# A gated cross-attention layer with routed experts: constants, buffers, a scaling step and PSUM banks moved

## Chip, core and metric

The kernel runs on one core of a Trainium2 chip. The metric is the device time of one execution in microseconds (us); lower is better. A core has TensorE for matmuls (PE in the profile, with its weight loads as PEld), VectorE (DVE), ScalarE (ACT), GpSimd (POOL) and SyncE (SP), which here only issues DMAs. Each engine works through its own queue in order; semaphores hold an instruction until what it needs is there. SBUF is the memory on the core; PSUM takes the results of matmuls, in eight banks of 512 fp32 values a partition.

## What is computed

For 8 batches of 512 tokens of width 256, one layer in fp32: attention of the normalized tokens `x` over a context of 512 keys with 16 heads of 16, masked, then a mixture of 8 experts of which each token takes 2. Both parts are added to `x` through a gate.

```python
x = x + tanh(g_xattn[0]) * attn(layernorm(x), ctx_1024, ctx_1024, mask, wq, bq, wk, bk, wv, bv, wo, bo)
x = x + tanh(g_ffn[0]) * ffn(layernorm(x), router_w, router_b, expert_up, expert_down)

# attn
scores = einsum("bhqd,bhkd->bhqk", q, k) / sqrt(16)
scores = where(mask == 0, -1e9, scores)
out = einsum("bhqk,bhkd->bhqd", softmax(scores), v) @ wo.T + bo
# ffn
probs = softmax(x_flat @ router_w + router_b)
top_w, top_idx = top_k(probs, 2)
output = sum over e of comb[:, e] * (gelu(x_flat @ expert_up[e].T) @ expert_down[e].T)
```

The drawn mask keeps the same keys, fewer than 128 in a row, for every query; the kernel finds this out on the chip and then attends only to a window of 128 keys.

## The kernel before

**The mask stage** (lines 95 to 585) loads the mask (`mask_i`, L98) and the first batch's tokens, makes constants on VectorE and POOL, and counts the dropped keys: `dropped` (L434, VectorE), its sum over rows `n_ps` (L446, TensorE), `act` (L447). From `act` and the constants `ahead` (L397, L398, made of `keys`) it reduces the first key `first` (L452) and the place of the window, `window_i` (L459), which SP reads into a register for the DMA of the keys' window (`load_window`, L467). `here`, `kept`, `diag`, `row_ps`, `drop` and `pick` (L490 to L503) describe which keys of the window count. `near_i` (L523) says whether the window covers all kept keys. Meanwhile `norms_0` measures the first batch's tokens: `look` (bn_stats, L209) and `settle` (L214 to L230, twelve small operations in a chain that ends in `rstd_end` and `shift`). Batch 0's projections end the stage: `kv_ps` (L537), `xnT_ps` (L259), `k_ps` (L549), `q_ps` (L568). The temporaries of this stage (`mask_i`, `dropped`, `xnT_0` and others) lie in the pool `mk`, which is given back at its end. A pool that is allocated over such memory makes its first users wait until the last reader of the old tiles is done.

A branch on `near_i` (L1349) then chooses `attend_near`, which is all that runs here; the other side, `attend_anywhere`, doesn't run.

**Pools of `attend_near`** (L806 to L823), in order of allocation in SBUF: `p2` (tokens `x`, windows `win`, `xnT`, weights' transposes `pT` and others), `small`, an empty pool `hold`, and then those that `experts` makes (`plan`, `weights`, `gather`, `hT`). In PSUM: `ps_s` with 4 banks (scores `t_ps` and `w_ps`, and the experts' `h_ps`), `ps_g` with 2 (everything else: `kv_ps`, `xnT_ps`, `q_ps`, `top_ps`, `proj_ps`, `bias_ps`, `o_ps`), `ps_o` with 2 (head outputs `n_av`, and `x_ps`, the transposed rows of an expert group).

**Rounds.** A loop over b from -1 to 7 (L1036) runs four groups g in each round, each for a half c of the heads and one parity i. In a group: `weights_T` (L891, four matmuls `w_ps` into four banks, each read by ScalarE's Exp, L903), `weigh` of the group before (L908: `n_av`, then VectorE's transpose `raw`, L922, and a division), `find_tops` of the next batch (L859: eight matmuls `t_ps` into four banks, each read by VectorE's max `tops`, L873), and `lower_tops` (L880: `top_ps`, then `ql`, L887). Between them stand the steps that `between` (L952) hands out by group and place `(g, n)`: projections of batch b+2, statistics and settle of b+3, output projection (`project_out`, L933) and routing (`route`, L304) of b-1. `scale_out` (L836) multiplies the output weights `woT` and bias `bo` by the gate: two matmuls into `bias_ps` (L844) with `bv_rows` (L843) as weights, and VectorE's L845, L847 and L846. `add_bias` (L849) adds `bo` to a batch's `x` on POOL (L850). Both run first at the end of round -1.

```python
if new == 1:
    put(3, 2, scale_out, lambda: add_bias(0))
put(*((3, 2) if new == 1 else (2, 0)), bias)
```

`new` is the batch that is being prepared, b+2 in round b; it is 1 in round -1.

**Experts.** Routed tokens are sorted into groups of 256 rows of one expert. Each group gathers its rows from DRAM (`xg`, L706), turns them (`x_ps`, L722, copied to `xT` by VectorE, L724), goes up (`h_ps`, L734, Gelu on ScalarE, L738) and down (`o_ps`, L752), is added to gathered rows of the output (`y`, L755) and scattered (L758). `plan` (L600) makes tables of which group is whose; its first instruction on VectorE is a memset of `groups` (L627). Some groups run within rounds 4 to 7 (`amid`, L1012), the rest in a loop after them.

**Order.** The program is written in order, and the scheduler of the tile framework may move an instruction on its engine where data allow it; `keep_in_program_order` pins one. SP's DMAs keep their order: mask, weights, first window, small constants, then window and tokens of batches 1 and 2, a clear of the routing table, and further tokens and windows.

Of the kernel before, what the change touches and what calls it, by code (L numbers as in the profile page):

```python
# [10 lines left out]
F32 = mybir.dt.float32  # L11
# [4 lines left out]
ALU = mybir.AluOpType  # L16
AX = mybir.AxisListType
PSUM = bass.MemoryType.PSUM

P = 128  # L20
B, S, D = 8, 512, 256
H, DH = 16, 16
# [4 lines left out]
EPS = 1e-5  # L27
# [36 lines left out]
def flamingo_layer(ctx: ExitStack, tc: tile.TileContext, a: dict, out: bass.AP):  # L64
    nc = tc.nc
# [5 lines left out]
    def fixed(shape, name, dtype=F32):  # L71
        return const.tile(shape, dtype, tag=name, name=name)
# [102 lines left out]
    ones_b = mk.tile([P, P], BF16, tag="ones_b", name="ones_b")  # L175
    nc.vector.memset(ones_b, 1.0)

    filled = keep.tile([P, E], F32, tag="filled", name="filled")
    nc.vector.tensor_scalar(filled, iota, float(TOKENS), None, ALU.mult)

# [13 lines left out]
    def measure(small, jobs, pin=False):  # L194


        nm = "_".join(f"{which}{b}" for b, which in jobs)
        n = len(jobs) * QT
        said = {}

        def column(name, i=0):
            return small.tile([P, 2 * QT], F32, tag=name, name=f"{name}_{nm}_{i}", bufs=3)[:, :n]

        def look(k):
            if "mv" not in said:
                said["mv"] = small.tile([P, 2 * QT, 2], F32, tag="mv", name=f"mv_{nm}", bufs=2)
            for t in range(QT):
                st = small.tile([P, 6], F32, tag="st", name=f"st_{nm}_{k}_{t}", bufs=4)
                ins = nc.vector.bn_stats(st, xs[jobs[k][0]][:, t, :])  # L209
                if t == 0 and pin:  # L210
                    tc.keep_in_program_order(ins)
                nc.vector.bn_aggr(said["mv"][:, k * QT + t, :], st)

        def settle():  # L214
            mv = said["mv"]
            v = column("var")
            nc.vector.tensor_scalar(v, mv[:, :n, 1], EPS, None, ALU.add)
            y = column("rstd")
            nc.vector.tensor_scalar(y.bitcast(I32), v.bitcast(I32), -0.5, RSQRT_MAGIC, ALU.mult, ALU.add)
            for i in range(3):  # L220
                yy = column("yy", i)
                nc.vector.tensor_tensor(yy, y, y, ALU.mult)
                hv = column("hv", i)
                nc.vector.scalar_tensor_tensor(hv, yy, -0.5, v, ALU.mult, ALU.mult)
                y2 = column("rstd", i + 1) if i < 2 else column("rstd_end")
                nc.vector.scalar_tensor_tensor(y2, hv, 1.5, y, ALU.add, ALU.mult)
                y = y2
            shift = column("shift")
            nc.vector.scalar_tensor_tensor(shift, mv[:, :n, 0], -1.0, y, ALU.mult, ALU.mult)
            said["rstd"], said["shift"] = y, shift  # L230

        return said, [lambda k=k: look(k) for k in range(len(jobs))], settle
# [178 lines left out]
    qs = [fixed([P, DC, S], f"q{i}") for i in range(2)]  # L411
    ks, kms = ([fixed([P, DC, 2, WINDOW], f"{n}{i}") for i in range(2)] for n in ("k", "km"))

    vals = [fixed([P, H, 2 * DH], f"nv{i}") for i in range(3)]
    for t in vals:
        nc.vector.memset(t[:, :, DH:], 1.0)

    act = mk.tile([P, S], F32, tag="act", name="act")
    first = fixed([P, 1], "first")
    window = fixed([P, 1], "window")  # L420
# [2 lines left out]
    with early, tc.tile_pool(name="ps_mask", bufs=1, space=PSUM) as ps_mask:  # L423
# [13 lines left out]
        norms_0 = measure(const, [(0, "a")], True)  # L437
# [35 lines left out]
        for dst, src in (  # L473
# [6 lines left out]
            (bv, a["bv"].partition_broadcast(P)),  # L480
        ):
            tc.keep_in_program_order(nc.sync.dma_start(out=dst, in_=src))
        norms_0[2]()

# [19 lines left out]
        for i in range(2):  # L506
            ins = nc.vector.tensor_scalar(bks[:, i, :], bk, half[:, 1 - i : 2 - i], None, ALU.mult)
# [298 lines left out]
    def attend_near(att):  # L806

        pool = lambda name, bufs, **kw: att.enter_context(tc.tile_pool(name=name, bufs=bufs, **kw))
        p2 = pool("near2", 2)
        small = pool("near_small", 4)  # L810
        hold = pool("near_hold", 1)
        ps_s = pool("near_ps_s", 4, space=PSUM)
        ps_g = pool("near_ps_g", 2, space=PSUM)
        ps_o = pool("near_ps_o", 2, space=PSUM)

        def bank(name):
            return ps_g.tile([P, 512], F32, tag="g", name=name)

        layernorms, finish = shared(p2, small, bank)
        plans, list_rows, fetch, load, turn_rows, ups, fetch_y, downs, compute, compute_extra = experts(  # L820
            pool, [b * S for b in PARTS], lambda name: ps_s.tile([P, 512], F32, tag="s", name=name), bank,
            lambda name: ps_o.tile([P, 512], F32, tag="av", name=name),
        )  # L823

        def held(shape, name, dtype=F32):
            return hold.tile(shape, dtype, tag=name, name=name)

        wins = {}

# [19 lines left out]
        def add_bias(b):  # L849
            nc.gpsimd.tensor_tensor(xs[b], xs[b], bo.unsqueeze(1).to_broadcast([P, QT, D]), ALU.add)  # L850
# [101 lines left out]
        def between(old, new, next_):  # L952

            plan = {(g, n): [] for g in range(4) for n in range(3)}

            def put(g, n, *steps):
                plan[g, n] += steps

            jobs = []
            if old is not None:
                x2T, keep_x, keep_rows, logits, route, place = finish(old)
                jobs.append((old, "f", x2T))
            if next_ is not None:
                xnT[next_] = None
                jobs.append((next_, "a", lambda: xnT[next_]))
            if jobs:
                looks, settle = normalize(*jobs)
            if new is not None:  # L970
                keys_values, keys_T, keys_less, bias, queries = prepare(new)
                _, scales, turns = normal[new, "a"]
                put(0, 2 if new == 1 else 0, keys_values)
                put(0, 1, *scales)
                put(1, 1, *turns, keys_T)
                put(3, 0, keys_less)
                put(2, 0, queries[0])
                put(2, 1, queries[1])
                if new == 1:
                    put(3, 2, scale_out, lambda: add_bias(0))  # L980
                put(*((3, 2) if new == 1 else (2, 0)), bias)
            if next_ is not None:
                put(0, 2, looks[-1])
            if old is not None:
                rows_f, scales, turns = normal[old, "f"]
                put(0, 1, lambda: project_out(old, (0, 1)))
                put(1, 0, lambda: project_out(old, (2, 3)), keep_x)
                put(1, 1, looks[0])
            if jobs:
                put(1, 2, settle)  # L990
            if old is not None:
                put(2, 0, *scales)
                put(2, 2, lambda: keep_rows(rows_f()))
                put(3, 0, *turns)
                put(3, 1, logits)
                put(3, 2, route)
                place, *enter = place
                counts = [count for count, end in zip(plans, PARTS) if old + 1 == end]
                later.append((place, enter, counts))
            return plan  # L1000
# [31 lines left out]
        looks, settle = normalize((1, "a", lambda: xnT[1]))  # L1032
# [3 lines left out]
        for b in range(-1, B):  # L1036
# [8 lines left out]
            if b == 0:  # L1045
                looks, settle = normalize((2, "a", lambda: xnT[2]))
# [11 lines left out]
            for g in range(4):  # L1058
                c, i = g // 2, g % 2
# [289 lines left out]
    with tc.If(is_near == 1) as which, ExitStack() as att:  # L1349
        attend_near(att)  # L1350
# [66 lines left out]
```

## Time and profile before

| | |
|---|---|
| device time, median of 3 runs | 852.25 us (850.71 to 857.43) |
| the profiled execution's own time | 827.52 us |
| its span, first to last instruction | 825.8 us |
| mean granted clock of TensorE | 0.974 |
| busy: PE, PEld | 763.0 us (92%), 571.9 us (69%) |
| busy: DVE, ACT, POOL | 317.8 us (38%), 252.6 us (31%), 313.6 us (38%) |
| TensorE, `h_ps` and `o_ps` together | 245.2 + 243.7 us |
| HBM | 147 GB/s over the span |

How to read it: the page's slices show each engine's busy share in tenths, over 40 equal parts of the span. The windows sum busy time in a stretch, with the number of instructions (x) and the granted clock (1.00 is full). A timeline line has start, length, engine (SPq is SP's queue), line of the kernel, operation, written and read tile, shape, count, and in brackets the idle time of the engine before it with what ended it. A matmul counts as busy while it waits in TensorE's pipeline, so a group of matmuls that takes longer than its like has waited.

### The profile page before, as it was taken

How to read it: one execution, taken by the hardware profiler on the slowest of the kernel's cores; microseconds unless marked ns; L12 is line 12 of the kernel's file. 1: busy time of each engine (PE TensorE's matmuls, PEld its weight loads, DVE VectorE, ACT ScalarE, POOL GpSimd, SP SyncE). 2: the span in 40 equal slices, each digit the busy share in tenths (PEclk: the TensorE clock that was granted, in tenths of full speed). 3: DMA queues.
4: the chain of work that ended last, by engine and by line, in shares of the span. 5: the costliest groups of instructions: out<-in, count | busy, mean ns of one | idle time of the engine just before them, and what ended most of it. 6: DMA issues, size and time to landing. Idle time of an engine off the chain costs nothing. (4 is left out here: it accounts for less than half of the span.)

```text
span 825.8 us, 11292 instructions
## 1 busy us (share of the span) xinstructions
PE 763.0 (92%) x4090; PEld 571.9 (69%) x4090; DVE 317.8 (38%) x958; ACT 252.6 (31%) x485; POOL 313.6 (38%) x422
## 2 busy tenths in 40 slices
PE   2788999998999899999996999999999999999992
PEld 1344545454465666768785888888898988989881
DVE  7468789888873565633320011111111101101100
ACT  1435475563644244442321121111211121111210
POOL 2021106244453251645464443443353433443331
PEclk9887999999999999999998999999999999999997
DMA  4610011120663214154548565665666775756511
GB/s 141 230 50 1 23 37 36 52 81 19 217 216 104 66 62 121 57 176 144 167 144 305 163 219 199 201 227 170 231 198 212 233 239 185 259 179 238 204 46 37
DMA packets 87909, 121.58 MB, mean 147 GB/s; under 512 B 16797, under 2 KB 71712, under 8 KB 87840
## 3 DMA queue, kind: packets, MB, share of 16 engines
q1 hardware_dynamic: 75184, 93.44, 33.8%
q0 software_dynamic: 11840, 26.76, 10.5%
q8 instruction: 36, 0.59, 0.3%
q10 hardware_dynamic: 816, 0.53, 0.2%
q14 instruction: 33, 0.27, 0.1%
HBM read 101.05 MB, written 20.17 MB: 147 GB/s over the span
## 5 line engine op out<-in xcount | busy, mean ns | idle before, releaser
L734 PE MATMUL h_ps<-xT,up 128*128 128x256 f32 (+1 forms) x1152 | 245.2, 370 | 5.9 <-DVE tops L873 4.3
L752 PE MATMUL o_ps<-down,hT 128*128 128x256 f32 x1088 | 243.7, 382 | 5.9 <-DVE y L755 5.5
L734 PEld LDWEIGHTS h_ps<-xT,up 128*128 128x128 f32 x1152 | 209.7, 191 | 35.7 <-DVE tops L873 5.1
L752 PEld LDWEIGHTS o_ps<-down,hT 128*128 128x128 f32 x1088 | 205.4, 192 | 37.1 <-DVE y L755 5.7
L738 ACT ACTIVATE hT<-h_ps 128x512 f32<-128x512 f32 (+1 forms) x144 | 82.2, 573 | 362.4 <-PE h_ps L734 362.3
L755 DVE SCALAR_TENSOR_TENSOR y<-o_ps,listed,y 128x256 f32<-128x256 f32 x68 | 32.7, 483 | 271.6 <-DMA y<-out,listed 133.3
L706 POOL DMA_INDIRECT y<-out,listed x68 | 66.1, 972 | 162.4 <-DMA out<-y,listed 130.6
L758 POOL DMA_INDIRECT out<-y,listed x68 | 68.8, 1012 | 95.6 <-DVE y L755 62.1
L873 DVE TENSOR_REDUCE tops<-t_ps 128x4 f32<-128x512 f32 x128 | 79.4, 680 | 18.2 <-PE t_ps L868 18.2
L903 ACT ACTIVATE n_pT<-w_ps 128x512 f32<-128x512 f32 x128 | 67.4, 598 | 44.4 <-PE w_ps L898 44.2
L706 POOL DMA_INDIRECT xg<-rows,listed x68 | 65.2, 958 | 40.4 <-issue 17.2
L372 POOL DMA_INDIRECT table<-entries,place_i x64 | 62.7, 979 | 25.9 <-issue 16.4
L898 PE MATMUL w_ps<-ql,km 32*128 32x512 f32 x256 | 62.8, 655 | 3.9 <-DVE tops L873 3.9
L724 DVE COPY xT<-x_ps 128x512 f32<-128x512 f32 (+1 forms) x36 | 23.6, 657 | 105.3 <-PE x_ps L722 105.3
L868 PE MATMUL t_ps<-k,q 32*128 32x256 f32 x512 | 43.9, 416 | 3.0 <-DVE tops L873 2.2
L868 PEld LDWEIGHTS t_ps<-k,q 32*128 32x128 f32 x512 | 27.1, 191 | 25.3 <-issue 15.0
L850 POOL TENSOR_TENSOR x<-x,bo 128x1024 f32<-128x1024 f32 x8 | 18.7, 2348 | 65.7 <-ACT xn_a L249 36.8
L898 PEld LDWEIGHTS w_ps<-ql,km 32*128 32x128 f32 x256 | 24.8, 187 | 19.7 <-DVE tops L873 15.0
L922 DVE STREAM_TRANSPOSE raw<-n_av 128x512 f32<-128x512 f32 x32 | 22.8, 712 | 34.3 <-PE n_av L916 34.3
L916 PE MATMUL n_av<-n_pT,nv 128*32 128x512 f32 x256 | 35.0, 619 | 0.0
L937 PE MATMUL proj_ps<-woT,oT 128*128 128x256 f32 x128 | 32.9, 392 | 1.6 <-DVE oT L930 1.5
L568 PE MATMUL q_ps<-n_xnT,wqT 128*128 128x512 f32 x64 | 32.9, 641 | 0.0
(187 smaller groups left out, 542.0 us busy)
## 6 DMA issues: line engine op xcount, KB each, us to landing
up<-in_upT SPq DMA_DIRECT2D x36, 1024.0 KB, 7.7
down<-in_downT SPq DMA_DIRECT2D x36, 1024.0 KB, 6.3
out<-x SPq DMA_DIRECT2D x8, 512.0 KB, 3.1
rows<-xn_f SPq DMA_DIRECT2D x8, 512.0 KB, 3.8
x<-in_x SPq DMA_DIRECT2D x7, 512.0 KB, 5.3
table<-none SPq DMA_DIRECT2D x1, 2288.0 KB, 11.0
xg<-rows,listed POOLq DMA_INDIRECT x68, 4.3
y<-out,listed POOLq DMA_INDIRECT x68, 2.8
```

The lines of the kernel that those rows point to most:

```text
L372: nc.gpsimd.indirect_dma_start(out=table_parts[2 * t + i][:, :], out_offset=bass.IndirectOffsetOnAxis(ap=place_i[:, t, i : i + 1], axis=0) ...
L568: nc.tensor.matmul(ps, lhsT=w["wqT"][:, dc, c * P : (c + 1) * P], rhs=xnT[:, dc, :], start=(dc == 0), stop=(dc == DC - 1),)
L706: nc.gpsimd.indirect_dma_start(out=dst, out_offset=None, in_=src[: seen[JOBS[s][0]], :], in_offset=bass.IndirectOffsetOnAxis(ap=listed[:, ...
L734: nc.tensor.matmul(ps[:, i, :n], lhsT=up[:, dc, (f + i) * P : (f + i + 1) * P], rhs=xT[:, dc, :n], start=(dc == 0), stop=(dc == DC - 1),)
L738: nc.scalar.activation(made[s][:, f : f + 2, :n], ps[:, :, :n], AF.Gelu)
L752: nc.tensor.matmul(ps, lhsT=hT[:, f, h * P : (h + 1) * P], rhs=down[:, f, :], start=(f == 0), stop=(f == FC - 1))
L758: nc.gpsimd.indirect_dma_start(out=out_parts[h][:, :], out_offset=bass.IndirectOffsetOnAxis(ap=listed[:, n, h, 0:1], axis=0), in_=y[:, h, ...
L868: ins = nc.tensor.matmul(ps[j][:, u], lhsT=q[rows_j, c, t * P : (t + 1) * P], rhs=k[rows_j, c], start=True, stop=True)
L873: nc.vector.tensor_reduce(top[:, 2 * tp : 2 * tp + 2, :].rearrange("p t (i x) -> p t i x", i=2)[:, :, :, 32 * j], ps[j], AX.X, ALU.max,)
L898: ins = nc.tensor.matmul(ps[j], lhsT=km[rows_j, c, i, :], rhs=lowered[b, c][rows_j, i, :], start=True, stop=True)
L903: nc.scalar.activation(pT[:, j, :], ps[j], AF.Exp)
L916: ins = nc.tensor.matmul(av[32 * j : 32 * j + 32, :], lhsT=made_of(b)[3][:, 8 * c + 2 * j + r, :], rhs=pT[:, j, :], start=True, stop=True,)
```

## The change

Three things move, and two pool sizes change:

1. The buffers `vals` and their memsets are made beside the early constants, and the settle of the first batch's statistics is pinned to program order. In the changed program's order on VectorE, the constants (`iota_e`, `filled`, `half`, `own`, `keys`, `ahead`, `less`) stand ahead of the first `dropped`, `first` and `window_i` follow `act` directly, and all twelve operations of settle come after `window_i`. On TensorE the first half of `kv_ps` stands ahead of `row_ps`.
2. In `attend_near` the experts' pools are allocated first, then `p2` and `small`; the empty `hold` goes. The experts' buffers now lie over the mask stage's temporaries.
3. `scale_out` moves from the end of round -1 to `(0, 2)` of round 0, with `add_bias` of batches 0 and 1 at `(1, 0)` and `(1, 2)`; batch 2's stays at `(2, 0)` of that round. In TensorE's order, `bias_ps` stands ahead of the second group's `w_ps`, with two of the third batch's transposes between its two halves.
4. `ps_s` has 5 banks, `ps_o` has 1.

SP's and POOL's queues keep their order of instructions.

```diff
@@ mask stage
+    vals = [fixed([P, H, 2 * DH], f"nv{i}") for i in range(3)]
+    for t in vals:
+        nc.vector.memset(t[:, :, DH:], 1.0)
+
     filled = keep.tile([P, E], F32, tag="filled", name="filled")
...
-        def settle():
+        def settle(pin=False):
             mv = said["mv"]
             v = column("var")
-            nc.vector.tensor_scalar(v, mv[:, :n, 1], EPS, None, ALU.add)
+            ins = nc.vector.tensor_scalar(v, mv[:, :n, 1], EPS, None, ALU.add)
+            if pin:
+                tc.keep_in_program_order(ins)
...
-    vals = [fixed([P, H, 2 * DH], f"nv{i}") for i in range(3)]
-    for t in vals:
-        nc.vector.memset(t[:, :, DH:], 1.0)
-
...
-        norms_0[2]()
+        norms_0[2](True)
@@ attend_near
-        p2 = pool("near2", 2)
-        small = pool("near_small", 4)
-        hold = pool("near_hold", 1)
-        ps_s = pool("near_ps_s", 4, space=PSUM)
+        ps_o = pool("near_ps_o", 1, space=PSUM)
         ps_g = pool("near_ps_g", 2, space=PSUM)
-        ps_o = pool("near_ps_o", 2, space=PSUM)
+        ps_s = pool("near_ps_s", 5, space=PSUM)
...
-        layernorms, finish = shared(p2, small, bank)
         plans, list_rows, fetch, load, turn_rows, ups, fetch_y, downs, compute, compute_extra = experts(
...
-        def held(shape, name, dtype=F32):
-            return hold.tile(shape, dtype, tag=name, name=name)
+
+        p2 = pool("near2", 2)
+        small = pool("near_small", 4)
+        layernorms, finish = shared(p2, small, bank)
@@ between
-                if new == 1:
-                    put(3, 2, scale_out, lambda: add_bias(0))
-                put(*((3, 2) if new == 1 else (2, 0)), bias)
+                if new == 2:
+                    put(0, 2, scale_out)
+                    put(1, 0, lambda: add_bias(0))
+                    put(1, 2, lambda: add_bias(1))
+                if new > 1:
+                    put(2, 0, bias)
```

## Prediction

> **What bounds the kernel now.** I read the slices of the page first: they tell where a change can pay.
>
> ```profile
> span 825.8 us, 11292 instructions
> ...
> PE   2788999998999899999996999999999999999992
> PEld 1344545454465666768785888888898988989881
> DVE  7468789888873565633320011111111101101100
> ```
>
> A slice is 20.6 us. From slice 20 on (about 400 us) TensorE is full and VectorE nearly idle: there only matmuls count, and the change removes none. In the first 350 us VectorE has 6 to 9 tenths and TensorE's nines are busy with waiting too. All three edits work there. Next the windows, for that first part:
>
> ```profile
> 20.00:30.00 10.00, 8.19 (x39) 4.59 (x38) 1.40 (x7) 5.58 (x13) 0.85 (x5) 1.00 0.22 65
> 30.00:40.00 10.00, 6.68 (x26) 3.09 (x24) 8.03 (x28) 2.76 (x6) 0.00 (x0) 0.80 1.05 368
> 40.00:50.00 10.00, 9.54 (x46) 4.90 (x48) 2.75 (x5) 4.22 (x10) 0.00 (x0) 0.69 0.44 136
> 60.00:70.00 10.00, 6.42 (x23) 2.71 (x25) 8.97 (x32) 4.46 (x8) 3.55 (x2) 0.67 0.00 0
> 100.00:150.00 50.00, 48.20 (x320) 24.65 (x323) 42.61 (x126) 31.55 (x68) 13.57 (x24) 1.00 0.18 57
> ```
>
> After the stretch come busy times of PE, PEld, DVE, ACT, POOL, then the granted clock. VectorE is idle 8.6 of 10 us at 20 to 30, and the clock falls twice. Then the timeline at those places:
>
> ```profile
> 26.82 0.39 SPq L467 DMA_DIRECT2D win<-in_ctxT  x1
> 26.92 0.42 DVE L843 TENSOR_SCALAR bv_rows<-ones,bvT 128x128 f32<-128x128 f32 x1 [5.87 <-PE q_ps L568]
> 27.33 0.95 SPq L86 DMA_DIRECT2D x<-in_x  x2
> 31.44 0.75 DVE L209 BATCH_NORM_STATS2 st_a<-x 128x6 f32<-128x256 f32 x2 [4.10 <-DMA x<-in_x]
> ...
> 56.56 4.65 POOL L850 TENSOR_TENSOR x<-x,bo 128x1024 f32<-128x1024 f32 x2 [28.89 <-DVE bo L846]
> 58.17 0.76 DVE L217 TENSOR_SCALAR var_a<-mv_a 128x4 f32<-128x4 f32 x1
> 58.96 2.27 DVE L219 TENSOR_SCALAR rstd_a<-var_a 128x4 int32<-128x4 int32 x1
> 63.85 3.01 PE L898 MATMUL w_ps<-ql,km 32*128 32x512 f32 x6 [3.58 <-DVE tops L873]
> ...
> 110.93 2.45 DVE L873 TENSOR_REDUCE tops<-t_ps 128x4 f32<-128x512 f32 x4
> 111.78 2.77 PE L898 MATMUL w_ps<-ql,km 32*128 32x512 f32 x8
> 115.61 0.72 DVE L922 STREAM_TRANSPOSE raw<-n_av 128x512 f32<-128x512 f32 x1 [1.59 <-PE n_av L916]
> ```
>
> First, `x1` is issued at 27.33, when the first batch's `q_ps` are done (26.62), although the branch's flag `near_i` was made at 20.52: its buffer lies over the mask stage's. Second, `rstd_a` takes 2.27 us where it takes 0.17 elsewhere, beside POOL's adds. Third, eight matmul records that take 1.14 us elsewhere take 2.77: each `w_ps` takes the bank of a `t_ps` whose `tops` is being read, one per 0.60 us.
>
> **What the Trainium skill says.** "SBUF — State Buffer", section "Who interferes with whom": a VectorE instruction that can take two ports (tensor_scalar, copy, cast), or that has two SBUF inputs while GpSimd reads SBUF, blocks against a GpSimd instruction for its whole length. The trace agrees: `rstd_a` ends with POOL's add (61.23 against 61.20), and `n_o`, two SBUF inputs, takes 1.74 us at 235.87 beside such an add against 0.42. "TensorE: Matmul & The Clock Gate", section "What's actually happening": an idle window of about 3.4 us halves the clock. The trace has half clock from 36.0 to 46.2 and 63.3 to 73.6, the second just after TensorE's 3.6 us wait; the threshold itself no run here shows. "PSUM — Partial Sum Buffer", section "Specifications (TRN2)": 8 banks of 512 fp32 a partition. So 5 + 2 + 1 uses all, and the fifth bank is taken from `ps_o`; the trace shows no bank count.
>
> **The change part by part.**
> *Constants ahead of the mask.* By start-to-start spacing, the eleven constants between 11.28 and 13.82 take 1.7 us of VectorE. They now stand ahead of the first `dropped` (3.83), from 2.3 on, where VectorE is idle 1.5 us before it and 1.5 us after. POOL works there without a pause; port waits bound the delay between 0 and 1.2 us (two memsets of `tops` at 1.05 each, part hidden). I take 0.4. Then `first` follows `act` (10.31) at once: `window_i` is ready at 11.9 instead of 14.41 and the window's load goes 2.4 us earlier. But now the first half of `kv_ps` (1.9 us of 3.75) stands ahead of `row_ps` on TensorE, and `drop`, `pick`, `kept`'s users and `near_i` wait behind it: `row_ps` ends at 15.1 + 1.9 + 0.8 = 17.8, not 17.04, so `near_i` comes 0.8 later, at 21.3. TensorE's chain to `q_ps` ends 1.7 us earlier, at 24.9. The pinned settle is the same twelve operations, and `here` keeps its 14.3.
>
> *Groups' buffers over first temporaries.* `p2` no longer lies over the mask pool, so SP's loads lose that wait. SP came through the branch in 0.6 us (20.55 to 21.11), so `x1` issues at 21.3 + 0.6 + 0.5 = 22.4 instead of 27.33 and, at the 4.1 us of before, lands at 26.5 instead of 31.4. The wait for `q_ps` isn't gone: the memset of `groups` now carries it, ahead of the statistics on VectorE, but ends by 25.0. So `x1`'s load stays last, and statistics start 4.9 us earlier. From there to `t_ps` at 45.83 one chain runs (statistics, `xn_a`, transposes, `q_ps`), so this carries. I count **4.7**, bounds 3.7 and 5.2. The table's clear (2,288 KB, issued at 29.02) and the later loads go earlier with it, on the same queue in the same order.
>
> *Output weights in round 0.* `scale_out` leaves the end of round -1: between `ql`'s end (53.74) and the next statistics (56.38) 2.6 us go, and `var_a`/`rstd_a` lose 0.6 + 2.1 = 2.7 us of port waits. VectorE's chain to `tops` at 63.11 gains about 5.1. In round 0 it all comes back: `bv_rows` 0.3, a wait for `bias_ps` of about 0.7 (0.60 for the matmul), `bo`, `woT`, `bo` 1.1. And now POOL has three adds ready at once, since the third batch's `xn_a` is done by then: 3 x 2.34 = 7.0 us without a pause. Settle of the next `x` stands in it: statistics fit under the first add, `var` waits for the first to end, `rstd` for the second, `yy` (two SBUF inputs) for the third. That is about 4.9 us lost; 2.1 + 4.9 = 7.0. Net on VectorE a loss of 1.9, of which some is slack (VectorE sat idle 0.9 and 1.35 before `ql` and `raw` at 75 to 77). I take a loss of **1.5**, bounds a loss of 4 and a gain of 1.6 (no third collision). Late next is `tops` for `w_ps` of group (1,0).
>
> *Five banks, one.* With five, `w_ps` number j waits for the reduce of `t_ps` j-1: 0.60 us less per group whose four start staggered. In the timeline 14 of 32 groups do. It pays where VectorE then idles for `n_av` (five groups: the one above, its like in rounds 2 to 4, the first of round 1) or TensorE is the bound (four, at 269 to 316): 9 x 0.60 = 5.4. In the other five, routing work covers it. In the main loop TensorE has no gap to fill. One bank for `n_av` and `x_ps` costs where they overlapped: `n_av` at 342.49 must wait for `xT` to end (344.17), but `h_ps` waits for that `xT` too, so 1.0; at 364.66 for 365.11, 0.5. Net a gain of **3.9**, bounds -1.5 and 7.
>
> *The sum.* 4.7 - 1.5 + 3.9 = 7.1 us, off the profiled execution's 827.52 (span 825.8 and 1.7 around it): 820.4. The runs' median, 852.25, lies 24.7 us above that; the profile doesn't show why, so I carry the saving over as it is: **845.1**.
>
> **The rivals.**
> *All of it at once, faster by over 1%.* `x1` comes early enough that TensorE has no idle window before 36 us, so the half clock there goes (`q_ps` 3.62 against 1.98, transposes 2.16 against 1.09, `k_ps` 1.22 against 0.71: 3.2 us), and every staggered group pays (14 x 0.6 - 1.5 = 6.9) while the scaling costs nothing: 4.7 + 3.2 + 6.9 = 14.8, 837.5. For: TensorE waits 2.2 us for `tops` at 33.7 and 1.15 for `xn_a` just before the fall. Against: the row-tiled matmuls there fill little of the array whenever they come.
> *The single output bank makes it slower.* `x_ps` holds its bank until VectorE copies `xT`, and VectorE's queue stands up to 19.5 us (133.3 in all) in `y` updates that wait for gathered rows. Three holds in rounds 4 to 7 are 5.1, 9.7 and 3.3 us; if `n_av` comes at the start of each, TensorE loses 18.1, net +11: 863. It decides once such waits pass 15.6 us (8.5 and the 7.1 gained). For: the bound stage hides nothing. Against: in before only 0.9, 1.7 and 0.5 us of these holds overlapped, and the order puts `x_ps` no earlier.
> *It doesn't do what it says.* The memset of `groups` is held by something later than `q_ps`, VectorE starts where it did, and 3.9 - 1.5 is left, less the 0.4 and 0.8 by which the flag is late: 851.
>
> **How the numbers follow.** About 1%, 8.5 us, is what a measurement here can tell from no change. The forecast has 0.44, the full gain 0.38, the single bank 0.12, the wait that stays 0.06. So faster 0.38, same 0.50 (forecast and last rival), slower 0.12. The range goes from 837 (the full gain) to 855: above it lies the single bank, below it almost nothing.
>
> **What would show it.** Right: `x1` issued near 22.4 and its statistics near 26.5; `groups`' memset ended by `q_ps`; `w_ps` groups near 2.2 us instead of 2.8; in round 0 three POOL adds in a row with a 2 us `rstd` and a slow `yy` beside them; no matmul at 350 to 420 waiting on `xT`. The prediction is wrong if the clock keeps full speed at 36 to 46 (then faster), if `near_i` slips past 22.5 (the load's gain shrinks), or if `n_av` or `x_ps` stands behind a `y` update (slower).

## The result, and the profile after

The changed kernel takes 848.74 us (median of 20 runs, 844.30 to 855.83) against 852.67 us before (848.04 to 857.43): a ratio of 0.9952, 95% interval 0.9932 to 0.9973, so 4.1 us or half a per cent faster. It was timed once more among the experiments: 0.9931, 0.9901 to 0.9961. The forecast was 845.1 us, 7.1 us faster; time fell by a little over half of that. The ratios leave out runs more than 1.5% above the fastest of their kernel, which count as slow, and the medians keep them; this matters for *banks 4 and 2* (5 of 22 left out), *buffers first* (9 of 22) and *constants late* (3 of 22), whose plain ratios of medians are 1.000, 0.9993 and 0.9928.

The profiled execution of the changed kernel is *longer* than the one shown of before, 848.9 us against 825.8. These two must not be subtracted. The first experiment profiled the kernel before again and got 853.1: the 825.8 was an unusually good execution, with less *half clock* (time in which the trace shows a granted clock of 0.5) than any other profile here. The lines of before that the prediction shows are of the first profile; from here on the changed kernel is compared with the second.

The slices of the page of the changed kernel (20 slices a side, as before; a slice is now 21.2 us):

```profile
span 848.9 us, 11331 instructions
...
PE   3786989888889999999997899999999999999992
PEld 1343544444446575668786788888898988788882
DVE  7486887877865747524230111101011101011100
```

The picture is the old one: VectorE busy and TensorE with gaps up to slice 20, then TensorE alone. The windows show the stretches that the prediction named, in the same order of columns:

```profile
20.00:30.00 10.00, 8.52 (x34) 3.69 (x34) 5.29 (x24) 4.78 (x12) 0.85 (x5) 1.00 0.70 233
30.00:40.00 10.00, 7.05 (x27) 3.86 (x26) 4.57 (x17) 4.65 (x10) 0.00 (x0) 0.58 0.95 317
40.00:50.00 10.00, 10.00 (x57) 5.11 (x56) 7.24 (x14) 4.23 (x8) 0.00 (x0) 0.91 0.00 0
60.00:70.00 10.00, 3.83 (x30) 1.58 (x22) 9.63 (x22) 3.48 (x8) 6.00 (x3) 0.84 0.00 0
100.00:150.00 50.00, 45.01 (x278) 21.76 (x277) 41.01 (x118) 29.06 (x62) 13.51 (x24) 0.93 0.14 47
```

VectorE works 5.3 us in 20 to 30 where it had 1.4 (1.3 in the second profile): the load came early, as forecast. But at 60 to 70 TensorE is busy 3.8 us instead of 6.4, and in 100 to 150 it has 45.0 us at a clock of 0.93, where before had 46.3 at 0.99 in its second profile and 48.2 at 1.00 in its first. The second is not in the forecast at all. The timeline of the changed kernel, at the places shown of before:

```profile
21.69 0.39 SPq L469 DMA_DIRECT2D win<-in_ctxT  x1
21.86 0.38 DVE L843 TENSOR_SCALAR bv_rows<-ones,bvT 128x128 f32<-128x128 f32 x1 [0.33 <-issue]
22.20 0.95 SPq L86 DMA_DIRECT2D x<-in_x  x2
23.85 0.06 DVE L629 MEMSET groups<- 128x1 f32 x1 [1.61 <-DMA win<-in_ctxT]
26.54 0.75 DVE L213 BATCH_NORM_STATS2 st_a<-x 128x6 f32<-128x256 f32 x2 [2.63 <-DMA x<-in_x]
...
57.70 2.09 PE L898 MATMUL w_ps<-ql,km 32*128 32x512 f32 x8
59.04 6.96 POOL L850 TENSOR_TENSOR x<-x,bo 128x1024 f32<-128x1024 f32 x3 [36.47 <-issue]
60.59 0.83 DVE L221 TENSOR_SCALAR var_a<-mv_a 128x4 f32<-128x4 f32 x1
61.46 2.27 DVE L225 TENSOR_SCALAR rstd_a<-var_a 128x4 int32<-128x4 int32 x1
63.76 2.25 DVE L228 TENSOR_TENSOR yy_a<-rstd_a 128x4 f32<-128x4 f32 x1
...
109.65 2.17 PE L898 MATMUL w_ps<-ql,km 32*128 32x512 f32 x8
...
122.27 2.34 POOL L850 TENSOR_TENSOR x<-x,bo 128x1024 f32<-128x1024 f32 x1 [1.48 <-ACT xn_a L255]
122.29 2.60 DVE L925 TENSOR_TENSOR n_o<-raw,inv 128x256 f32<-128x256 f32 x1
124.92 0.71 DVE L930 STREAM_TRANSPOSE oT<-n_o 128x512 f32<-128x512 f32 x1
125.69 1.59 PE L937 MATMUL proj_ps<-woT,oT 128*128 128x256 f32 x6 [3.07 <-DVE oT L930]
```

Down to 64 us this is the forecast, line by line: `x1` at 22.20 (22.4 was foretold), statistics at 26.54 (26.5), three adds in a row (6.96 us; 7.0), a slow `rstd_a` and a slow `yy_a`. The groups of `w_ps` at 57.70 and 109.65 take 2.09 and 2.17 us where 2.2 was foretold and 2.77 stood before. The last four lines are the surprise: in round 1 `n_o`, two SBUF inputs, takes 2.60 us for 0.43, because POOL's add of `bo` starts 0.02 us before it, and TensorE waits 3.07 us for `oT`. It comes back at 163.08 (2.61) and 204.37 (2.26). The waits of TensorE from 50 to 300 us (columns: total us, times, longest us), first before (second profile), then changed:

```profile
PE w_ps L898 <- DVE tops L873: 7.2, 4, 3.6
PE place_ps L342 <- DVE x L942: 3.4, 4, 1.0
PE h_ps L734 <- DVE oT L930: 3.1, 1, 3.1
...
PE proj_ps L937 <- DVE oT L930: 1.5, 4, 0.6
```

```profile
PE proj_ps L937 <- DVE oT L930: 9.2, 3, 3.1
PE k_ps L551 <- ACT n_xnT L266: 7.8, 3, 6.7
PE xnT_ps_a L265 <- DVE ql L887: 3.3, 1, 3.3
```

The waits of `w_ps` for `tops` are gone from the head of the list; three waits for `oT`, and one of 6.7 us for `n_xnT` behind the three adds, stand in their place.

### The profile page after: what moved, and what is told of

It is laid out like the page before. It is cut to its first block, busy times and chain, and to the rows that moved or that the text cites. A ratio compares the mean times of both kernels' runs of the same rounds, so it can differ in the third digit from the quotient of the medians.

```text
span 848.9 us, 11331 instructions
## 1 busy us (share of the span) xinstructions
PE 767.4 (90%) x4090; PEld 568.3 (67%) x4090; DVE 326.6 (38%) x958; ACT 253.6 (30%) x485; POOL 313.8 (37%) x422
## 3 DMA queue, kind: packets, MB, share of 16 engines
q0 software_dynamic: 11840, 26.76, 10.2%
## 5 line engine op out<-in xcount | busy, mean ns | idle before, releaser
L754 PE MATMUL o_ps<-down,hT 128*128 128x256 f32 x1088 | 245.2, 383 | 10.9 <-DVE y L757 9.6
L708 POOL DMA_INDIRECT xg<-rows,listed x68 | 64.9, 955 | 41.3 <-issue 17.7
L898 PE MATMUL w_ps<-ql,km 32*128 32x512 f32 x256 | 60.0, 714 | 0.6 <-DVE tops L873 0.6
L868 PE MATMUL t_ps<-k,q 32*128 32x256 f32 x512 | 40.8, 408 | 1.7 <-ACT q L574 0.8
L916 PE MATMUL n_av<-n_pT,nv 128*32 128x512 f32 x256 | 40.0, 701 | 1.7 <-DVE xT L726 1.7
L868 PEld LDWEIGHTS t_ps<-k,q 32*128 32x128 f32 x512 | 25.3, 189 | 23.8 <-issue 16.5
L937 PEld LDWEIGHTS proj_ps<-woT,oT 128*128 128x128 f32 x128 | 23.2, 192 | 20.8 <-DVE oT L930 11.4
```

The source lines that it names most:

```text
L708: nc.gpsimd.indirect_dma_start(out=dst, out_offset=None, in_=src[: seen[JOBS[s][0]], :], in_offset=bass.IndirectOffsetOnAxis(ap=listed[:, ...
L754: nc.tensor.matmul(ps, lhsT=hT[:, f, h * P : (h + 1) * P], rhs=down[:, f, :], start=(f == 0), stop=(f == FC - 1))
L868: ins = nc.tensor.matmul(ps[j][:, u], lhsT=q[rows_j, c, t * P : (t + 1) * P], rhs=k[rows_j, c], start=True, stop=True)
L898: ins = nc.tensor.matmul(ps[j], lhsT=km[rows_j, c, i, :], rhs=lowered[b, c][rows_j, i, :], start=True, stop=True)
L916: ins = nc.tensor.matmul(av[32 * j : 32 * j + 32, :], lhsT=made_of(b)[3][:, 8 * c + 2 * j + r, :], rhs=pT[:, j, :], start=True, stop=True,)
L937: nc.tensor.matmul(ps[:, t - ts[0], :], lhsT=outs[b, c][:, t * P : (t + 1) * P], rhs=w["woT"][:, c, :], start=(c == 0), stop=(c == DC - 1),)
```

## The experiments

The kernels were run in groups, each group on one chip beside the kernel before; the ratio is to those runs, so medians of different groups (before has 852.8, 856.1 and 856.4 us in the three) are not to be compared. A *lead* is how much earlier a TensorE instruction starts than in the second profile of before: at the third group of `t_ps` (46.11 us there), and at the first `proj_ps` of batches 0, 1, 3, 5 and 7 (94.39, 125.66, 202.45, 304.00 and 389.59 us). Batch 1's comes just ahead of the collision in round 1 (121.92 us in the changed kernel), so what the collisions cost shows from b1 to b3. Leads come from one execution each, so a microsecond of them means little.

| kernel | median us | ratio, 95% interval | third `t_ps` | b0 | b1 | b3 | b5 | b7 |
|---|---|---|---|---|---|---|---|---|
| changed | 848.74 | 0.9952 (0.9932-0.9973) | 5.2 | 2.3 | 3.7 | -1.2 | 6.5 | 9.2 |
| changed, again | 850.14 | 0.9931 (0.9901-0.9961) | 5.6 | 2.6 | 4.0 | 1.5 | 8.4 | 7.9 |
| before, again | 853.99 | 1.0008 (0.9981-1.0035) | 0 | 0 | 0 | 0 | 0 | 0 |
| banks 4 and 2 | 852.86 | 0.9979 (0.9952-1.0006) | 4.6 | 1.3 | 1.3 | 1.5 | 1.7 | 1.7 |
| scaling early | 844.44 | 0.9916 (0.9881-0.9951) | 5.9 | 7.4 | 8.8 | 3.1 | 10.3 | 11.0 |
| buffers first | 852.23 | 0.9964 (0.9933-0.9994) | 2.7 | 0.4 | 1.8 | -3.0 | 4.8 | 7.5 |
| constants late | 850.22 | 0.9917 (0.9894-0.9940) | 5.2 | 3.0 | 4.4 | -0.2 | 4.2 | 6.1 |
| adds in four | 846.33 | 0.9897 (0.9852-0.9942) | 5.9 | 3.3 | 4.7 | 3.4 | 10.8 | 12.7 |
| adds in four, banks 4 and 2 | 855.83 | 0.9994 (0.9973-1.0016) | 5.8 | 3.0 | 3.0 | 0.8 | 0.3 | 0.0 |
| scaling after the settle | 845.78 | 0.9882 (0.9855-0.9908) | 5.3 | 5.6 | 7.1 | 0.2 | 9.3 | 12.6 |
| adds in four, scaling early | 841.80 | 0.9846 (0.9796-0.9897) | 4.8 | 6.5 | 8.0 | 5.9 | 17.0 | 17.6 |
| adds in four, scaling after | 844.42 | 0.9876 (0.9844-0.9908) | 5.8 | 8.9 | 10.3 | 7.5 | 18.5 | 19.0 |

**The kernel before, once more.** No edit.

> The kernel before, unchanged. It asks whether the profile of before is typical. Theory (the profile of before was a lucky execution): 852.5 us, ratio 1.000; its clock in the timed executions is 0.95 to 0.96, not 0.974, and the profile has half-clock stretches of about 6.8 us in rounds 1 to 4 (100 to 260 us), as the changed kernel's has five of. Rival (the change itself brings these stretches): again a clock of 0.974 and none between 84 and 278 us.

Level, as it must be. Its profile:

```profile
span 853.1 us, 11292 instructions
...
PE   3879998989899899989999799999999999899992
```

Up to 140 us TensorE's matmuls follow the first profile within 0.7 us, but for 1.5 us in a half-clock stretch at 30 us that the first lacks, made up by 34 us. Then the granted clock of the trace falls to half at 149.2, 190.2, 227.7, 265.3, 296.0 and 367.7 us, for 3.4 or 6.8 us each, where the first had one such stretch (278.4). In all 75.8 us of its span are at half clock against 42.3. So the stretches in rounds 1 to 4 are no product of the change. With 33.5 us more of them the span is 27.3 us longer: TensorE is busy for 17.7 us more (780.7 for 763.0) and idle for 9.6 us more. The slower clock goes with most of the 24.7 us between the first profile and the median, but some 2 us are lost just ahead of the fall at 149.2, and what sets these stretches off is not shown.

**Four banks and two.** The fifth bank and the lost output bank, undone.

```diff
-        ps_o = pool("near_ps_o", 1, space=PSUM)
+        ps_o = pool("near_ps_o", 2, space=PSUM)
...
-        ps_s = pool("near_ps_s", 5, space=PSUM)
+        ps_s = pool("near_ps_s", 4, space=PSUM)
```

> The change with four banks for scores and two for head outputs, as before. The prediction's step 4 (the banks gain 3.9): 852.6, ratio to before 1.000. Rival (in the changed kernel's profile n_av waits 0.7 + 2.4 us for xT where 1.5 were counted, and the staggered groups give 2.5 us: the banks bring nothing): 848.5, ratio 0.995. A gain over the changed kernel (844 to 846, 0.990 to 0.993) would say that the single bank costs more than the fifth gives.

0.9979 lies between the two expectations, and its interval reaches from one to the other: by this run the banks are worth 2.3 us (0.0027 of 853) against the changed kernel's first timing and 4.1 against its second; by the ratios of medians it is 4 and 6. The forecast 3.9 lies among these, but the first comparison alone does not exclude that the banks bring nothing. The trace says more. With four banks there is no collision in rounds 1 to 3; batch 1's `n_o` is through before the add starts:

```profile
124.13 0.43 DVE L925 TENSOR_TENSOR n_o<-raw,inv 128x256 f32<-128x256 f32 x1
...
124.70 2.35 POOL L850 TENSOR_TENSOR x<-x,bo 128x1024 f32<-128x1024 f32 x1 [2.08 <-ACT xn_a L255]
125.36 1.56 PE L937 MATMUL proj_ps<-woT,oT 128*128 128x256 f32 x6 [0.31 <-DVE oT L930]
```

And its lead stays flat (1.3, 1.3, 1.5, 1.7), while the changed kernel's falls by 4.9 from batch 1 to 3 and rises by 7.7 from 3 to 5. So the banks seemed to do two large things of opposite sign.

**Scaling at the end of round -1 again.**

```diff
-                if new == 2:
-                    put(0, 2, scale_out)
-                    put(1, 0, lambda: add_bias(0))
-                    put(1, 2, lambda: add_bias(1))
-                if new > 1:
-                    put(2, 0, bias)
+                if new == 1:
+                    put(3, 2, scale_out, lambda: add_bias(0))
+                put(*((3, 2) if new == 1 else (2, 0)), bias)
```

> The change with the output weights scaled at the end of round -1 again. The prediction's step 3 (the move loses 1.5): 847.2, ratio 0.994. Rival A (round 0 loses more than was counted, since a second half-clock stretch goes with the three adds in a row: 55 to 62 and 69 to 76 us, TensorE's waits of 3.3 and 6.7 us): 842 to 844, ratio 0.988 to 0.990. Rival B (the move gains, since round -1 comes 4 us earlier and the rest is slack): 851 to 853, 1.000.

844.44, ratio 0.9916: between step 3 and rival A, nearer to A, and the interval holds both. The lead at batch 0 is 7.4 us against 2.3 and 2.6. In time the gain over the changed kernel is 0.0036, 3.1 us (0.0015 against its second timing), which the intervals do not separate; the next run on this point does.

**Scaling after the settle.** It stays in round 0, but behind the fourth batch's settle.

```diff
-                if new == 2:
-                    put(0, 2, scale_out)
-                    put(1, 0, lambda: add_bias(0))
-                    put(1, 2, lambda: add_bias(1))
-                if new > 1:
+                if new > 2:
                     put(2, 0, bias)
...
             if jobs:
                 put(1, 2, settle)
+            if new == 2:
+                put(1, 2, scale_out, lambda: add_bias(0))
+                put(2, 0, lambda: add_bias(1), bias)
```

> The change with the output weights scaled later in round 0, after the settle of the fourth batch's statistics. Theory (the loss of the move is the settle standing in three adds, not the work moved): var, rstd and yy take 0.17 each, 4 to 5 us come back, 843 to 845, ratio 0.989 to 0.991, like the scaling at the end of round -1. Rival (the loss is the 1.8 us of work and its wait for bias_ps, wherever it stands in round 0): 847 to 849.

0.9882 against 0.9952 and 0.9931: faster by 0.0070, give or take 0.0034, and by 0.0049, give or take 0.0040. The settle now runs at full speed:

```profile
57.35 0.17 DVE L221 TENSOR_SCALAR var_a<-mv_a 128x4 f32<-128x4 f32 x1
57.55 0.17 DVE L225 TENSOR_SCALAR rstd_a<-var_a 128x4 int32<-128x4 int32 x1
57.76 0.16 DVE L228 TENSOR_TENSOR yy_a<-rstd_a 128x4 f32<-128x4 f32 x1
```

The work moved is the same, in the same round: what cost time was where the three adds fell. The adds now meet one `n_o` instead (2.19 us at 73.45), and rounds 1 to 3 still collide: the lead goes from 7.1 to 0.2.

**The attention's buffers opened first again.**

```diff
+        p2 = pool("near2", 2)
+        small = pool("near_small", 4)
         ps_o = pool("near_ps_o", 1, space=PSUM)
...
-        p2 = pool("near2", 2)
-        small = pool("near_small", 4)
         layernorms, finish = shared(p2, small, bank)
```

> The change with the attention's working buffers opened ahead of the experts' again. The prediction's step 2 (the buffers alone give 4.7): x1's load is issued at about 25 us, when the last reader of the mask stage's buffers is done, not at 22.2, statistics start about 5 us later than 26.5, and the time is 853.4, ratio 1.001. Rival (what is gained ahead of the first round is given back in it or at a half-clock stretch): x1 as late, but within 1 us of the changed kernel, 849, ratio 0.996.

`x1` is issued at 25.20, statistics start at 29.02, and the lead at the third `t_ps` is 2.7 instead of 5.2 to 5.6: the buffers' share is there, half as large as was expected here, since the constants alone bring the end of the mask stage forward. In time it is not told from the changed kernel by these ratios (0.9964 against 0.9952); by the ratios of medians it is 3 to 6 us slower (0.9993 against 0.9954 and 0.9927), so this is not settled either.

**The constants where they were.**

```diff
-    vals = [fixed([P, H, 2 * DH], f"nv{i}") for i in range(3)]
-    for t in vals:
-        nc.vector.memset(t[:, :, DH:], 1.0)
-
...
+    vals = [fixed([P, H, 2 * DH], f"nv{i}") for i in range(3)]
+    for t in vals:
+        nc.vector.memset(t[:, :, DH:], 1.0)
+
     act = mk.tile([P, S], F32, tag="act", name="act")
...
-        norms_0[2](True)
+        norms_0[2]()
```

> The change with VectorE's constants and the first settle where they were before. With the attention's buffers opened first again, x1 was issued at about 24 us and the third group of t_ps came 2.7 us earlier than before instead of 5.2; so the two parts share the load's gain. Theory (the constants carry the other half, through the chain to q_ps that the memset of groups waits for): x1's statistics at about 28.5 to 29, t_ps of the third group 2.3 to 3 us later than the changed kernel's 40.9, ratio to before 0.997 to 0.999. Rival (the prediction's step 1: the constants move near_i 0.8 later and give nothing by themselves; the buffers carry the whole load): x1 at 22 us, within 1 us of the changed kernel, 0.995.

The theory of that expectation falls. `x1` is issued at 21.75 and the third `t_ps` comes at 40.93, level with the changed kernel's 40.92; the ratio is 0.9917 beside 0.9931 for the changed kernel in the same group. The timeline of this kernel shows the two waits in series:

```profile
21.75 0.95 SPq L86 DMA_DIRECT2D x<-in_x  x2
...
26.09 0.06 DVE L629 MEMSET groups<- 128x1 f32 x1 [4.31 <-PE q_ps L570]
26.61 0.75 DVE L209 BATCH_NORM_STATS2 st_a<-x 128x6 f32<-128x256 f32 x2 [0.46 <-DMA x<-in_x]
```

The memset waits for `q_ps`, later than in the changed kernel, but still ends half a microsecond before the data lands. With the buffers moved, the constants buy nothing that shows; without, they bring the third `t_ps` forward by 2.7 us. The two parts overlap.

**Each add cut into four.** The order on VectorE, ScalarE and TensorE is unchanged.

```diff
         def add_bias(b):
-            nc.gpsimd.tensor_tensor(xs[b], xs[b], bo.unsqueeze(1).to_broadcast([P, QT, D]), ALU.add)
+            for t in range(QT):
+                nc.gpsimd.tensor_tensor(xs[b][:, t, :], xs[b][:, t, :], bo, ALU.add)
```

> The change with each of POOL's adds of bo cut into four (128x256 instead of 128x1024); the order on VectorE, ScalarE and TensorE is that of the change. Theory (with five banks the attention runs far enough ahead that n_o, two SBUF inputs, meets POOL's add in rounds 1 to 3: 2.6, 2.6 and 2.3 us for 0.43, TensorE waits 9.8 us for oT; and in round 0 three adds hold var, rstd and yy 4.9 us): an instruction of VectorE waits for one short add, at most 0.65 us, so n_o takes about 1.0, rstd and yy 0.8 at most, some 3.5 us come back in round 0 and 4.8 in rounds 1 to 3, ratio to before 0.985 to 0.987, 840 to 842. Rival A (VectorE gets the port only when POOL's whole queue of adds is through): n_o 2.6 again, 848.5, 0.995. Rival B (n_o's wait is slack): n_o about 1.0, but 846 to 848.

0.9897: between the theory (0.985 to 0.987) and rival B, and the interval does not decide. It is faster than the changed kernel's first timing by 0.0055, give or take 0.0050, and not told from its second (0.0034, give or take 0.0054). Its timeline in rounds 0 and 1 (the first of the twelve pieces started before the window of the first line):

```profile
58.88 7.54 POOL L851 TENSOR_TENSOR x<-x,bo 128x256 f32<-128x256 f32 x11
...
60.35 0.65 DVE L225 TENSOR_SCALAR rstd_a<-var_a 128x4 int32<-128x4 int32 x1
61.03 0.64 DVE L228 TENSOR_TENSOR yy_a<-rstd_a 128x4 f32<-128x4 f32 x1
61.71 0.65 DVE L230 SCALAR_TENSOR_TENSOR hv_a<-yy_a,var_a 128x4 f32<-128x4 f32 x1
...
121.28 0.72 POOL L851 TENSOR_TENSOR x<-x,bo 128x256 f32<-128x256 f32 x1 [1.49 <-ACT xn_a L255]
121.30 0.98 DVE L926 TENSOR_TENSOR n_o<-raw,inv 128x256 f32<-128x256 f32 x1
...
123.08 1.56 PE L938 MATMUL proj_ps<-woT,oT 128*128 128x256 f32 x6 [1.45 <-DVE oT L931]
```

`n_o` waits for one short add (0.98), and the loss from batch 1 to 3 shrinks from 4.9 (2.5 in the second profile) to 1.4. But in round 0 nothing came back (lead 3.3 at batch 0, for 2.3 and 2.6): the two engines take turns, and each of ten settle operations waits for one piece, 0.57 to 0.65 us for 0.16. Cutting helps a single instruction, not a chain that lies under a whole queue of adds.

**Adds in four, four banks and two.** The two diffs above together.

> POOL's adds cut into four, and four banks for scores and two for head outputs; the rest as changed. It measures what the fifth bank is worth when no n_o meets an add. Theory (the fifth bank's own gain is some 2.5 us ahead of the fifth round and 4 after it, and its cost in the changed kernel was the port): 3 to 5 us slower than five banks with the adds cut, 844 to 846, ratio 0.990 to 0.992. Rival (the banks bring nothing by themselves): level with it, within 1 us.

0.9994 against 0.9897, a difference of 0.0097, give or take 0.0050. So five banks and one, in place of four and two, are worth about 8 us (4 to 13) once no long add is in their way, where 3 to 5 were expected. In the leads it shows late: from batch 3 to 5 the four-bank kernels gain 0.2 and -0.5, the five-bank ones 4.4 to 11.1. TensorE's waits from 245 to 304 us with four banks, and in the changed kernel:

```profile
PE h_ps L736 <- DVE oT L931: 3.2, 1, 3.2
PE w_ps L899 <- ACT hT L740: 2.3, 2, 1.9
PE h_ps L736 <- DVE tops L874: 0.8, 1, 0.8
```

```profile
PE h_ps L736 <- DVE oT L930: 1.7, 1, 1.7
PE place_ps L348 <- DVE x L942: 0.4, 1, 0.4
```

The experts' `h_ps` draw from the same banks as the scores, so there `w_ps` waits for `hT` and `h_ps` for `tops`. The three later profiles with four banks (before again and the two kernels here) also have two half-clock stretches in this part, at 264 to 265 and at 294 to 296 us, 6.8 us each; the changed kernel has none there, and 3.4 us at 294 in its second profile.

How much of this the banks themselves do is open. From batch 3's first `proj_ps` to batch 5's, these three four-bank profiles take 101.3 to 102.0 us, of which 13.7 to 20.5 are at half clock; the five-bank ones with all the work take 90.5 to 97.2, with 3.4 to 13.7. But before's first profile, which has four banks too, takes 91.3, with 3.4, and TensorE's idle time in the stretch is much alike in all of them (9.2 to 13.0 us). So most of the difference goes with the half clock, and one four-bank execution does without it. The 8 us are measured in time; that they come from waits for these banks is argued.

**Both repairs.** Adds in four with the scaling early, and with it after the settle.

> The change with the output weights scaled at the end of round -1 again and POOL's adds cut into four. Theory: it takes both gains, 844.4 less 4.8 in rounds 1 to 3 less 2 at the settle beside the first two adds: 838 to 840, ratio 0.983 to 0.985, and beats the change and before. Rival (rounds 1 to 3 give it back in TensorE's half-clock stretches): 843 to 845.

> The change with the output weights scaled after the fourth batch's settle and POOL's adds cut into four. Theory (the two repairs meet different collisions and add up: 0.7% in round 0, 0.5% in rounds 1 to 3): ratio to before 0.981 to 0.985, the fastest of all. Rival (what round 0 gives is lost again ahead of the fifth round, as with the scaling moved alone, whose lead of 5.6 us was 0.2 at 168 us): 0.988.

0.9846 and 0.9876: both are faster than the changed kernel, by 5 to 9 us as its two ratios have it, and neither is told from the other. The first is where its theory had it (0.983 to 0.985); the second misses its own (0.981 to 0.985) and has the rival's number, though not its reason, since its lead is kept (18.5 us at batch 5). The second has the longest lead at the end of the attention (19.0 us) and, but for before's first, the shortest profile (833.8 us), but no better time than scaling after the settle alone (0.9882): its own gain in time is not shown.

**No adds.** POOL's adds are left out.

```diff
         def add_bias(b):
-            nc.gpsimd.tensor_tensor(xs[b], xs[b], bo.unsqueeze(1).to_broadcast([P, QT, D]), ALU.add)
+            pass
```

> The changed kernel without POOL's adds of bo to x; the bias of the output projection is left out. The order on the other engines is the change's. It bounds what all of POOL's adds cost the changed kernel. Theory (4.9 us in round 0 and 6.5 in rounds 1 to 3, of which most is on the path): var, rstd, yy 0.17, n_o 0.43, ratio 0.980 to 0.984. Rival (POOL's adds are only the messenger, and VectorE's order sets these rounds): 0.992 or more.

898.66 us, 1.0517, and neither theory had that. Without the bias the tokens are routed differently (72 gathers of rows instead of 68), and from the last `proj_ps` to TensorE's last matmul it takes 501 us instead of 444, with waits of up to 13.6 us for gathered rows. Only the attention can be read, and from round 4 on with care, since experts' groups run within it: its leads are 10.2, 11.7, 10.9, 18.0 and 16.8 us at batches 0, 1, 3, 5 and 7. There `var`, `rstd`, `yy` and `n_o` take 0.17, 0.17, 0.16 and at most 0.46 us. At batch 3 that is 9.4 to 12.1 us more than the changed kernel, which bounds what the adds cost up to there; the two repaired kernels get back 4.5 to 8.7 of it. At batch 7 they are no longer behind (17.6 and 19.0).

**The changed kernel again.** No edit.

> The changed kernel once more, beside the other three on the same chip. All theories: ratio to before 0.993 to 0.997; n_o at about 2.6 us in rounds 1 to 3 and TensorE waiting some 9.8 us for oT, as in its first profile. If n_o took 0.43 here, the collision would be a chance of one execution.

0.9931, and `n_o` at 2.60, 2.60 and 2.26 us in rounds 1 to 3: no chance of one execution. The windows from 112 to 136 us, over round 1's collision, here and with the adds in four:

```profile
112.00:136.00 24.00, 20.38 (x141) 10.62 (x137) 18.60 (x51) 8.98 (x21) 7.08 (x17) 0.86 0.02 7
```

```profile
112.00:136.00 24.00, 21.01 (x169) 11.62 (x167) 21.31 (x63) 11.24 (x26) 7.59 (x19) 1.00 0.10 30
```

All six profiles in which a whole add meets `n_o` have a half clock in this window (0.79 to 0.93), beginning within 1.5 us of the end of TensorE's wait of 3.1 us for `oT`, on either side of it; the seven later profiles without it, where that wait is 1.5 us at most, have 1.00. But the length of the wait doesn't decide alone: of the twelve equal waits in rounds 2 and 3 of the same six profiles, two have a fall within 1.5 us. "TensorE: Matmul & The Clock Gate" of the Trainium skill, section "What's actually happening", has an idle window of about 3.4 us behind such a fall. The falls measured here do not all fit that: the one at 151.0 us of the changed kernel comes after 3.4 us in which TensorE has no idle time in the trace, and before's second profile falls at 227.7 us after 0.7 us of it.

## Why the prediction was half right

**Constants ahead of the mask: right.** `window_i` was ready at 12.05 (11.9 was foretold), `near_i` at 21.00 and, in the second profile, 21.19 (21.3). No gain was given to this part, and it has none beside the buffers.

**Groups' buffers: right.** 4.7 was counted; the lead at the third `t_ps` is 5.2 and 5.6, and 5.2 with this part and without the constants. The memset of `groups` ended at 23.9 and 25.3 (25.0), ahead of the data.

**Scaling in round 0: the mechanism right, the size too small.** A loss of 1.5 was taken. The three adds in a row, the wait of `var` for the first, `rstd` for the second and `yy` for the third came exactly so, and VectorE's own sum held: the lead of `tops` grew from 5.1 us at the group before to 10.5 at the one that the prediction named (5.4 for 5.1) and fell to 3.3 at the next (7.2 lost, for 7.0). What failed is "of which some is slack". TensorE could use only part of the early gain (from the third `t_ps` to the first `n_av` its lead grew by 3.2 and 3.1 us), and from there to the first `proj_ps` it lost 6.1 us: over both its lead went from 5.2 to 2.3, where with the scaling early it went from 5.9 to 7.4. That is a loss of about 4.4 at the end of round 0, just beyond the bounds, of which 1 to 6 us show in the time (0.0036 and 0.0070, or 0.0015 and 0.0049 against the second timing). The half clock goes with it, 13.7 and 17.1 us of it between 50 and 80 us against 6.8 with the scaling early, as that run's rival A had it. (The prediction read the fall of before at 63.3 us as coming "just after" a wait of 3.6 us; it began 0.5 us before that wait ended.)

**Five banks, one: the net near, its path wrong.** A gain of 3.9 was forecast, 5.4 less 1.5; the run gives between 2.3 and 6 without settling it. The gain that was counted, 0.60 us for each of nine staggered groups, left out that `h_ps` shares these banks: from batch 3 to 5 the lead grows by 4.4 to 11.1 us where 2.4 were counted, most of it with the half clock, and with the adds cut the banks are worth some 8 us. The single bank cost about the 1.5 us that was said: `n_av` waits once for `xT`, 1.7 us and 2.3 us in the two profiles, and never behind a `y` update. But "no matmul at 350 to 420 waiting on `xT`" is wrong, since this wait ends at 359. What failed here is the sentence "In the other five, routing work covers it": in rounds 1 to 3 being earlier was not free. It brought `n_o` 0.02 us behind the start of an add, and with it three waits of 3.1 us for `oT` and, in round 1, a half-clock stretch, in place of a gain. The profile of before had shown the pattern, `n_o` at 1.74 us beside such an add at 235.87; the prediction used it as evidence for the rule and did not ask which other `n_o` stood close to an add.

**The sum.** 4.7 - 1.5 + 3.9 met a lead of 5.2 to 5.6 us, a loss of 1 to 6 in time and a gain of 2.3 to 6, which is too coarse to add up; measured were 4.1 in all, between 2.3 and 5.8. That the total came within 3.6 us of the forecast is in part luck: the collisions, which it did not have, and the gain from batch 3 on, which it counted too small, lie on opposite sides. Carrying the saving over to the median, and not the profiled span, was right for a reason that the prediction did not have: its profile lacked 33.5 us of half clock.

**The rivals.** *All of it at once* fell because the clock still halves, only sooner (at 31.5 to 41.8 us; 34.7 to 41.5 in the second profile), and because of the collisions. *The single bank* fell because its one wait is 1.7 to 2.3 us, far from the 15.6 from which it decides. *It doesn't do what it says* fell with `x1` at 22.20.

**Open.** Both profiles of the changed kernel take 444 us from the last `proj_ps` to TensorE's last matmul, the second of before 440.6, so some of the lead of 8 to 9 us is lost in the experts' loop. TensorE's waits after 700 us, all for `y`, don't explain it (3.3 and 2.6 us against 2.7), and other kernels with the same loop take from 437.8 to 444.1. No run was aimed at it, nor at what starts a half-clock stretch.

## What to carry to other kernels

A change that makes one engine earlier also moves it against every other engine's work: before counting a gain, list VectorE's instructions that a trace has shown waiting for GpSimd's, and ask which of their like will lie within one long GpSimd instruction after the change. Long GpSimd instructions that nothing waits for are best cut short where one instruction of VectorE may meet them, and kept away altogether from a chain of short ones. And where the profiled execution and the median differ by 3%, take a second profile before reading small stretches out of the first.

## What was not expected of the hardware

- Under a queue of short GpSimd adds VectorE gets one instruction through after each: ten settle operations took 0.57 to 0.65 us for 0.16 each. Under three long adds only three of them waited, for 4.9 us in all; the whole settle was as long either way. "SBUF — State Buffer" of the Trainium skill, section "Who interferes with whom", has the blocking, which this agrees with; the taking of turns is what the trace adds. `hv_a` (SCALAR_TENSOR_TENSOR) waits as well.
- Two executions of one kernel differed by 27.3 us in span and by 33.5 us in time at half clock (825.8 and 42.3, 853.1 and 75.8), though 140 us into it they were still within 0.7 us of each other.
